# One averaging product per group norm, an earlier range count, and moved fill-in work in the last stretch of a four-layer kernel

## The chip, the cores and the metric

The kernel runs on one core of a Trainium2 chip. The time is the device time of one launch in microseconds (us); the figure compared is the median of several runs. Before the change it was 2970.94 us (three runs, 2970.92 to 2973.89). Names used below: PE is the matrix engine (TensorE), DVE the vector engine, ACT the scalar engine, POOL the GpSimd engine, SP the engine that issues most DMAs. A bank is one 128 x 512 float32 piece of PSUM, the accumulator memory that PE writes; there are eight.

## What is computed

Four images of 256 channels and 64 x 64 pixels go through four layers. Every layer adds f(group_norm(x)) to x, with groups of 8 channels. Cut to what matters:

```python
# layer 0: 3x3 convolution, group norm of 8 groups (32 channels each), relu, non-local attention, a second such norm
xs = relu(group_norm(conv3x3(xn) + smooth_b, gn1_w, gn1_b))
attn = softmax(theta(xs) @ phi(xs))            # 4096 x 4096 for each image
x = x + group_norm(conv1x1(attn @ g(xs), w_w) + w_b, gn2_w, gn2_b) * 0.1 + xs
# layer 1: rmsnorm, linear attention with 4 heads, rmsnorm
# layer 2: a small network makes a depthwise 3x3 kernel and a 1x1 kernel from the image itself
# layer 3: softmax over 4 experts mixes a 1x1 kernel
def _gn(v, G=32, eps=1e-5):                    # in front of every layer
    m = mean(group(v)); s = var(group(v))
    return (v - m) / sqrt(s + eps)
```

The softmax of layer 0 is taken without a running maximum. So the kernel counts on the way whether every sum and its reciprocal stayed in range, and a general version runs behind it if one did not.

## The kernel before

`conv_preact_fast` works on one image at a time, both halves of 128 channels (`NH = 2`) side by side on 128 partitions. While image b is in the attention of layer 0 (`attend`, L986), which keeps PE dense with products `pf` (L1013) and `py` (L1126, L1129), the other layers of image b-1 and the convolution of image b+1 are threaded into it step by step (`Chain`, L50, and the calls at L1989 to L1998). The program order on every engine is the order in which these Python generators emit: `tc.manual_schedule` (L1986) keeps it. Each engine runs its own list in order and waits on semaphores.

Two stretches have nothing beside them. The first image's convolution and norm (`convolve_first`, L863; `normed_relu`, L745) come before any attention. And the last image's layers 0 to 3 (`tail`, L1948, with `xs_in` and `diag` set, so that `alone` is true in the helpers) come after all of it. There the kernel fills PE's waits in two ways:

- **Held products.** The 16 pieces of image 2's layer 3 (`mixed`, L1927 to L1930) are not issued when they are ready but kept in a list, and `w.fill(n)` (L58) issues the next n: per piece four matrix passes of 512 columns (`ps_ex` L1907). `w.settle()` later issues their evictions on ACT, and these the stores on SP. All 16 have to be issued somewhere.
- **Dummies.** `warm(n)` (L350) issues 2n products of 128 x 128 of constants, four passes for each n, whose result nobody reads.

A group norm needs per-channel means and variances (`bn_stats` and `bn_aggr` on DVE, or sums that ACT and DVE accumulate on the way), then the average over the channels of a group. `group_finish` (L396) takes two products for that, one after the other: `pm` averages the means over the group (`avg32` or `avg8`, a block-diagonal matrix), DVE forms variance plus squared deviation from that mean, `pv` averages it, and POOL takes the power -0.5 (`rsqrt`, L230). Five such norms lie in the two lonely stretches: in `normed_relu` for image 0, and for the last image in `nonlocal_out` (L1152, whose statistics of the layer-0 sum are worked out from those of its parts: `wmv`, `res_mv`, `joint`), in `linear_attention` (L1261), in `generated` (L1521) and in `mixed` (L1840).

What surrounds them in the last image: `ended` (L1074) turns the last block of the attention (`ps_yt`, L1091), projects it (`ps_wy`, L1101) and takes its statistics (`wy_st`, L1030). At L2010 the loop over the rest of the attention's steps issues held products after the first of them. `linear_attention` runs eight blocks that transpose and project, forms the context (`ps_ctx`), turns it into one matrix `w2` by three small products (L1386 to L1402), and applies it in `outputs`, eight blocks, each adding into `big` with `bn_stats` beside it (`added`, L1439). `generated` plans its depthwise taps over four engines (`emit_by_start`, L1496). Its last sums are accumulated by `added` on DVE (L1769) and `square` on ACT (L1774). `mixed` then finds the mixing weights: norm, `ps_hid`, `ps_log`, softmax, `wm` on DVE, and the 16 final products with evictions on ACT and DVE and stores on SP.

At the very end, outside, `conv_preact_kernel` (L2518) compares the collected `guard` values (`fit`, `low`), counts over the partitions by a product (`count`, L2536), makes an integer (`good`), loads it into a register of each engine (L2538) and branches around the general version (L2539). The list order on DVE lets `fit` and `low` run early, but `count` stands behind the last final product.

Of the kernel before, what the change touches and what calls it, by code (L numbers as in the profile page):

```python
# [13 lines left out]
P = 128  # L14
# [89 lines left out]
def conv_preact_fast(ctx: ExitStack, tc: tile.TileContext, guard, x, wc, wtpg, ww, wqkv, wout, w1cat, wd2,  # L104
# [252 lines left out]
    def sums_tile():  # L357
        return sp.tile([P, 2, NH, N // 512], F32, name="sums", bufs=1)
# [21 lines left out]
    def accumulated(sums, pivot, parts=N // 512):  # L380

        both = sp.tile([P, 2, NH], F32, name="both_m", bufs=1)
        mv = sp.tile([P, NH, 2], F32, name="mv")
        if parts == N // 512:
            nc.vector.tensor_reduce(both, sums, AX.X, ALU.add)
        else:
            nc.vector.tensor_reduce(both[:, 0, :], sums[:, 0, :, 0:parts], AX.X, ALU.add)
            nc.vector.tensor_reduce(both[:, 1, :], sums[:, 1, :, :], AX.X, ALU.add)
        nc.vector.tensor_scalar(both, both, 1.0 / N, None, ALU.mult)
        tt(pivot, pivot, both[:, 0, :], ALU.add)  # L390
        tt(pivot, pivot, pivot, ALU.mult)
        tt(mv[:, :, 1], both[:, 1, :], pivot, ALU.subtract)
        nc.vector.tensor_copy(mv[:, :, 0], both[:, 0, :])
        return mv

    def group_finish(st, avg, eps, shift=None, between=(), idle=(0, 0)):  # L396
# [34 lines left out]
        return mv, gm, rstd  # L431

# [312 lines left out]
    def normed_relu(b, st, hops=0):  # L745
# [4 lines left out]
        _, gm, rstd = yield from group_finish(st, avg32, 1e-5, bias, (), (0, 0) if b else (7, 1))  # L750
        if b == 0:
            warm(5)
# [110 lines left out]
    def convolve_first(w):  # L863
# [59 lines left out]

        for oh in range(NH):
# [3 lines left out]
            nc.vector.tensor_scalar(minus[:, oh:oh + 1], pivot[:, oh, 0:1], -1.0, None, ALU.mult)  # L928
            for k in (1, 2):
                for i, f in enumerate((AF.Identity, AF.Square)):  # L930
                    nc.scalar.activation(k4("about").rearrange("p (y x) -> p y x", x=HW), image[:, oh, :, k, :], f,
                                         bias=minus[:, oh:oh + 1], accum_out=sums[:, i, oh, k - 1:k])
        for i, (y, ps) in enumerate(y3):
            tt(y, y, ps, ALU.add)
            if i == NH:
                half(0, 3)
        half(1, 3)

        yield from normed_relu(0, lambda: joined_moments(st, sums, minus))
# [32 lines left out]
    pivot_in = cp.tile([P, NH], F32, name="pivot_in")  # L972
    last_block, res_mv = [], []
# [4 lines left out]
    def residual_known():  # L978
# [5 lines left out]
        tt(res_shift, res_mv[0][:, :, 0], factors[:, 1, :], ALU.add)  # L984

    def attend(b):  # L986
# [8 lines left out]
        def with_residual(q, wt, xc):  # L995

            if q == 0:
# [3 lines left out]
                nc.vector.tensor_scalar(pivot_in, mv[:, :, 0], -1.0, None, ALU.mult)  # L1001
            if q < NQ - 1:
# [149 lines left out]
    def nonlocal_out(w, b, big, k4, xs_in):  # L1152
# [22 lines left out]
        wmv, gm, rstd = yield from group_finish(wy_stats[b], avg32, 1e-5, bias, between, (0, 0) if xs_in is None else (2, 1))  # L1175
# [6 lines left out]
        if xs_in is not None:  # L1182


            mean = sp.tile([P, NH, 1], F32, name="mean_in", bufs=1)
# [5 lines left out]
            rmv = res_mv[0]  # L1191
            tt(off, wmv[:, :, 0], pivot_in, ALU.add)
            tt(off, off, bias, ALU.subtract)
            nc.vector.tensor_reduce(cov, joint, AX.X, ALU.add)
            tt(off, off, rmv[:, :, 0], ALU.mult)
            stt(cov, cov, 1.0 / N, off, ALU.mult, ALU.subtract)
            tt(off, wmv[:, :, 0], gm, ALU.subtract)
            tt(sc, rstd, factors[:, 0, :], ALU.mult)
            tt(off, off, sc, ALU.mult)
            tt(mean[:, :, 0], off, res_shift, ALU.add)  # L1200
            w.fill(1)

            def variance():
                tt(var, wmv[:, :, 1], sc, ALU.mult)
                stt(var, cov, 2.0, var, ALU.mult, ALU.add)
                tt(var, var, sc, ALU.mult)
                tt(var, var, rmv[:, :, 1], ALU.add)
                return var
# [25 lines left out]
            return (lambda: (mean, variance)), (sh, shift), on_the_way()  # L1234
# [26 lines left out]
    def linear_attention(w, b, big, qT, k4, st, sh, sums):  # L1261

        alone = sums is not None
        if alone:
# [6 lines left out]
            _, gm, rstd = yield from group_finish(st, avg8, 1e-5, None, (lambda: next(sums), at_last), (0, 1))  # L1271
# [88 lines left out]
        for c in range(NC):  # L1360
            if c + 1 < NC:
                ahead = normed(c + 1)
            if alone:
                next(sums, None)
            elif b + 2 < B and c % 2 == 0:
                copy_x(b + 2, c // 2)
# [20 lines left out]
        for h in range(NH):  # L1387
            nc.tensor.transpose(pt[:, bass.ts(h, P)], cx[:, bass.ts(h, P)], ident)
        cxT = k2("cxT")[:, 0:NH * P]
# [3 lines left out]
        for h in range(NH):  # L1393
            nc.tensor.matmul(pe[:, 0:P], wqkv_s[:, h, 2 * HID:3 * HID], cxT[:, bass.ts(h, P)], start=(h == 0), stop=(h == NH - 1))
        cmT = k2("cmT")[:, 0:P]
# [4 lines left out]
        nc.tensor.matmul(pw[:, 0:NH * P], cmT, wout_s, start=True, stop=True)  # L1400
        w2 = k2("w2")[:, 0:NH * P]
# [46 lines left out]
        if alone:  # L1448

            this, last = outputs(0), None  # L1450
            root(this[0])
            for c in range(NC):
# [4 lines left out]
                if last is not None:  # L1457
                    added(c - 1, last)
                this, last = after, z
                w.settle()  # L1460
                if c in (2, 4):
# [5 lines left out]
            return st  # L1467
# [53 lines left out]
    def generated(w, b, big, k4, st, sh, diag):  # L1521
# [4 lines left out]
        mv, gm, rstd = yield from group_finish(st, avg8, 1e-5, sh, (), (0, 0) if diag is None else (0, 1))  # L1526
        if diag is not None:
            w.fill(1)

        pivot = sp.tile([P, NH], F32, name="pivot", bufs=1)  # L1530
        tt(pivot, sh, mv[:, :, 0], ALU.subtract)
# [66 lines left out]
        sums = sums_tile()  # L1598

        def st():  # L1600
            return accumulated(sums, pivot)
# [231 lines left out]
        else:  # L1833
            yield from halves_of_three()
        sh2 = sp.tile([P, NH], F32, name="sh2")
# [4 lines left out]
    def mixed(w, b, big, k4, st, sh, held):  # L1840
# [4 lines left out]
        alone = held is None and b == B - 1  # L1845
        if alone:
            w.fill(1)
        mv, gm, rstd = yield from group_finish(st, avg8, 1e-5, sh, (), (0, 1) if alone else (0, 0))
        if alone:
            warm(2)  # L1850
        off = sp.tile([P, NH], F32, name="off")
        tt(off, gm, sh, ALU.subtract)
        pool = sp.tile([P, NH], F32, name="rpool", bufs=1)
        tt(pool, mv[:, :, 0], gm, ALU.subtract)
        tt(pool, pool, rstd, ALU.mult)
# [20 lines left out]
        w.fill(3)  # L1876

        scales = sp.tile([P, NH, NE], F32, name="scales", bufs=1)
        for h in range(NH):
            nc.vector.tensor_scalar(scales[:, h, :], al, rstd[:, h:h + 1], None, ALU.mult)  # L1880
# [66 lines left out]

    def tail(b, big, qT, k4=k4, diag=None, xs_in=None, held=None):  # L1948
# [37 lines left out]
    with tc.manual_schedule(engines={E.PE, E.Activation, E.DVE, E.Pool, E.SP}):  # L1986
# [23 lines left out]
        for part, _ in enumerate(attention):  # L2010
            if part == 0:
                end.fill(2)
# [505 lines left out]
def conv_preact_kernel(ctx: ExitStack, tc: tile.TileContext, *args):  # L2518
# [4 lines left out]
    conv_preact_fast(tc, guard, *args)  # L2523


    fit = gp.tile([P, 2, B * NQ + 1], F32, name="fit")
    for side in range(2):
        nc.vector.tensor_scalar(fit[:, side, :], guard[:, side, :], GUARD_MAX[side], None, ALU.is_le)
    low = gp.tile([P, 1], F32, name="low")
    nc.vector.tensor_reduce(low, fit.rearrange("p s k -> p (s k)"), AX.X, ALU.min)  # L2530
    every = gp.tile([P, 32], F32, name="every")
    nc.gpsimd.memset(every, 1.0)
    good = gp.tile([32, 1], mybir.dt.int32, name="good")
    with tc.tile_pool(name="guard_ps", bufs=1, space=bass.MemoryType.PSUM) as gps:
        count = gps.tile([32, 1], F32, name="count")
        nc.tensor.matmul(count, every, low, start=True, stop=True)  # L2536
        nc.vector.tensor_scalar(good, count, P - 0.5, None, ALU.is_ge)
    in_range = nc.values_load(good[0:1, 0:1], min_val=0, max_val=1)  # L2538
    with tc.If(in_range < 1):  # L2539
# [59 lines left out]
```

## Time and profile before

| what | us |
|---|---|
| median of three runs | 2970.94 (2970.92 to 2973.89) |
| the profiled execution's own time | 2974.19 |
| its span, first to last instruction | 2972.4 |
| PE busy | 2918.3 (98%) |
| DVE, ACT, POOL busy | 1785.9, 1352.4, 187.1 |
| first image's last row product to first projection (`ps_tp`) | 130.4 to 140.2 |
| last image alone, from the turn of its last attention block to the last product | 2732.8 to 2964.3 |
| from the last product to the end of the span | 8.1 |

The profile is of one execution. Its span leaves out 1.8 us of its own time. Busy times of PE come from modelled ends of pipelined passes: in a dense stream a pass of 512 columns starts every 0.43 us, one of 128 columns every 0.11 us at full clock. The granted clock is a record of its own, in fractions of full speed. A group of instructions in the timeline is given by start, duration, engine, source line, operation, tiles written and read, and, where the engine stood idle before it, how long and what released it. Helpers such as `tt` (L137) and `stt` (L140) give all their instructions one line, so that a DVE operation is best followed by its tiles.

### The profile page before, as it was taken

The numbers are of one execution on the slowest core, as the hardware profiler recorded it, in microseconds if no ns is written. First come the engines' busy times: TensorE is split into PE (matmuls) and PEld (weight loads), VectorE is DVE, ScalarE is ACT, GpSimd is POOL, SyncE is SP. The second block draws the span as 40 slices with busy tenths as digits, with TensorE's granted clock in tenths as the row PEclk, the third lists the DMA queues.
The fourth block names the chain that finished last, engine by engine and source line by source line (L and its number), as shares of the span: only waits on it lengthen the run. The fifth ranks groups of instructions, "written<-read, shape, count | busy, mean of one in ns | idle before, by whom it ended". The sixth has DMA issues, their size and how long they took to land.

```text
span 2972.4 us, 31260 instructions
## 1 busy us (share of the span) xinstructions
PE 2918.3 (98%) x11604; PEld 1776.5 (60%) x11604; DVE 1785.9 (60%) x2793; ACT 1352.4 (45%) x2717; POOL 187.1 (6%) x225
## 2 busy tenths in 40 slices
PE   7999999999999999999999999999999999999998
PEld 3454555556566666777566666677646544446744
DVE  8737757751545853675355584567244558863584
ACT  2234333345656444225665544323656554433773
POOL 0000000001001000000011000000001100000152
PEclk9999999999999999999999999999999999999999
DMA  6245444324322012121630302211431233235121
GB/s 228 73 87 120 70 62 76 45 32 100 114 39 36 29 78 75 53 62 28 156 75 4 58 7 107 68 50 57 83 102 14 25 43 39 32 58 116 36 71 72
DMA packets 371296, 199.38 MB, mean 67 GB/s; under 512 B 305664, under 2 KB 315648, under 8 KB 367616
## 3 DMA queue, kind: packets, MB, share of 16 engines
q1 hardware_dynamic: 71328, 175.81, 17.6%
q10 hardware_dynamic: 295200, 4.72, 8.0%
q0 software_dynamic: 4608, 16.78, 3.8%
q8 instruction: 93, 1.52, 0.2%
q14 instruction: 67, 0.55, 0.1%
HBM read 131.18 MB, written 82.87 MB: 72 GB/s over the span
## 4 chain that ended last, share of the span: by engine, by line
PE 78%; issue 16%; DVE 3%; ACT 2%; DMA 1%; POOL 0%; SPq 0%; DVEq 0%; ACTq 0%; POOLq 0%
PE pf L1013 24%; PE py L1129 16%; PE py L1126 8%; PE ps_tp L951 4%; PE ps_qk L1316 3%; PE ps_ex L1907 3%; PE ps_pw L1620 3%; PE ps_conv L663 2%; PE ps_ctx L1343 2%; PE ps_o L1414 2%; PE ps_g L956 2%; PE ps_row L617 1%; PE ps_conv L578 1%; PE ps_wy L1066 1%; ACT big L760 1%
## 5 line engine op out<-in xcount | busy, mean ns | idle before, releaser
L1014 ACT ACTIVATE pr<-pf 128x512 f32<-128x512 f32 x1024 | 602.3, 596 | 911.7 <-PE pf L1013 888.9
L1013 PE MATMUL pf<-tpg 128*128 128x512 f32 x2048 | 966.4, 594 | 0.0
L1013 PEld LDWEIGHTS pf<-tpg 128*128 128x128 f32 x2048 | 374.1, 190 | 358.4 <-issue 336.4
L1129 PE MATMUL py<-pr,tpg 128*128 128x512 f32 x1152 | 541.6, 592 | 0.9 <-ACT pr L1014 0.9
L1126 PEld LDWEIGHTS py<-tpg,pr 128*128 128x128 f32 x3584 | 434.9, 192 | 108.0 <-issue 100.7
L1126 PE MATMUL py<-tpg,pr 128*128 128x129 f32 x3584 | 436.3, 275 | 2.3 <-ACT pr L1014 2.3
L1129 PEld LDWEIGHTS py<-pr,tpg 128*128 128x128 f32 x1152 | 218.6, 190 | 277.5 <-issue 268.3
L137 DVE TENSOR_TENSOR tot<-tot,pr 128x1024 f32<-128x1024 f32 x252 | 307.5, 1220 | 98.6 <-ACT pr L1014 98.1
L140 DVE SCALAR_TENSOR_TENSOR dw<-xp,dk,dw 128x1008 f32<-128x1008 f32 x192 | 242.9, 1270 | 7.6 <-ACT dw L1612 2.4
L663 PE MATMUL ps_conv<-v,u 128*128 128x256 f32 x864 | 195.6, 379 | 2.4 <-DVE v L137 2.4
L663 PEld LDWEIGHTS ps_conv<-v,u 128*128 128x128 f32 x864 | 161.5, 190 | 31.4 <-issue 8.4
L232 POOL TENSOR_TENSOR rstd<-rstd,half 128x2 f32<-128x2 f32 x24 | 17.5, 730 | 2093.8 <-DVE rstd L427 1983.4
L951 PE MATMUL ps_tp<-big,wtpg_s 128*128 128x512 f32 x256 | 116.7, 595 | 4.0 <-ACT big L760 4.0
L137 DVE TENSOR_TENSOR tpg<-ps_g,bg_s 128x512 f32<-128x512 f32 x32 | 22.1, 691 | 155.6 <-PE ps_g L956 155.6
L1316 PE MATMUL ps_qk<-wqkv_s,xg 128*128 128x256 f32 x496 | 113.6, 379 | 0.0
L140 DVE SCALAR_TENSOR_TENSOR sums<-ps_conv,sums 128x512 f32<-128x512 f32 x72 | 49.7, 691 | 104.0 <-PE ps_conv L663 97.6
L1316 PEld LDWEIGHTS ps_qk<-wqkv_s,xg 128*128 128x128 f32 x496 | 93.8, 190 | 20.3 <-issue 8.4
L1620 PE MATMUL ps_pw<-dw,pk 128*128 128x512 f32 x192 | 86.3, 592 | 0.0
L951 PEld LDWEIGHTS ps_tp<-big,wtpg_s 128*128 128x128 f32 x256 | 45.9, 190 | 53.4 <-issue 42.1
L952 ACT ACTIVATE tpg<-ps_tp,btp_s 128x512 f32<-128x512 f32 x64 | 44.0, 687 | 70.8 <-PE ps_tp L951 70.8
L1079 DVE COPY total<-py 128x2 f32<-128x2 f32 x28 | 4.5, 159 | 115.6 <-PE py L1126 115.6
L1915 ACT ACTIVATE res<-ps_ex,b 128x512 f32<-128x512 f32 x56 | 38.1, 686 | 75.3 <-PE ps_ex L1907 74.4
(412 smaller groups left out, 3351.6 us busy)
## 6 DMA issues: line engine op xcount, KB each, us to landing
u<-filters SPq DMA_DIRECT2D x72, 256.0 KB, 2.8
xp<-in_x_dram SPq DMA_DIRECT2D x16, 1024.0 KB, 8.3
xs_d<-big POOLq DMA_DIRECT2D x32, 512.0 KB, 6.3
wy_d<-wt SPq DMA_DIRECT2D x32, 512.0 KB, 2.8
wy<-wy_d SPq DMA_DIRECT2D x32, 512.0 KB, 4.9
out_dram<-res SPq DMA_DIRECT2D x64, 256.0 KB, 2.0
xs_d<-in_x_dram SPq DMA_DIRECT2D x24, 512.0 KB, 6.7
xs<-xs_d SPq DMA_DIRECT2D x24, 512.0 KB, 5.5
```

What stands on the lines that cost most here:

```text
L137: nc.vector.tensor_tensor(o, a, b, op)
L140: nc.vector.scalar_tensor_tensor(o, a, s, b, op0, op1)
L663: nc.tensor.matmul(ps[:, bass.ts(oh, IY * IX)], u[i][:, h, bass.ts(oh, P)], v[:, i, bass.ts(h, IY * IX)], start=(h == 0), stop=(h == NH - 1))
L951: nc.tensor.matmul(ps, wtpg_s[:, h, k, :], big[:, h, cols], start=(h == 0), stop=(h == NH - 1))
L956: nc.tensor.matmul(ps[:, j, :], big[:, h, bass.ts(4 * c + j, P)], wtpg_s[:, h, 2, :], start=(h == 0), stop=(h == NH - 1))
L1013: nc.tensor.matmul(pf, phi[:, bass.ts(2 * m + s, P)], theta[:, bass.ts(q, 512)], start=True, stop=True)
L1014: nc.scalar.activation(pr[:, bass.ts(s, 512)], pf, AF.Exp)
L1126: nc.tensor.matmul(py[t // 2][:, t % 2, :], probs[i][:, s * 512 + t * P:s * 512 + (t + 1) * P], g[:, 2 * m + s, :], start=(begin and t % 2 ...
L1129: nc.tensor.matmul(py, g[:, 2 * m + s, 0:P], probs[i][:, bass.ts(s, 512)], start=begin, stop=end)
L1316: nc.tensor.matmul(ps[:, 0:2 * HID], xg[:, h, bass.ts(j, P)], wqkv_s[:, h, 0:2 * HID], start=(h == 0), stop=(h == NH - 1))
L1620: nc.tensor.matmul(ps, pk[:, h * NH * P + oh * P:h * NH * P + (oh + 1) * P], dw[h][:, bass.ts(s, 512)], start=(h == 0), stop=(h == NH - 1))
L1907: nc.tensor.matmul(ps, wm[h][:, bass.ts(oh, P)], big[:, h, bass.ts(c, 512)], start=(h == 0), stop=(h == NH - 1))
```

## The change

Five norms get one averaging product in place of two. `group_once` and `group_known` put mean and variance-plus-square into one tile, both taken about a value that all channels of a group have in common (`centre`), and average the two in one product. Group variance is then the averaged square minus the square of the averaged mean. The common value is averaged earlier by a small product of its own: from the first quarter of the image in `convolve_first`, from the first block in `attend` and in the outputs of layer 1, and from the residual's mean in `residual_centred`.

```diff
+    def group_known(both, centre, avg, eps, between=(), idle=0):
+        yield None
+        warm(idle)
+        pm = bank("pm")
+        nc.tensor.matmul(pm[:, 0:2 * NH], avg, both.rearrange("p k h -> p (k h)"), start=True, stop=True)
+        for f in between[0:1]:
+            f()
+        sq = sp.tile([P, NH], F32, name="sq_g", bufs=1)
+        nc.vector.tensor_copy(sq, pm[:, 0:NH])
+        tt(sq, sq, sq, ALU.mult)
+        rstd = sp.tile([P, NH], F32, name="rstd")
+        stt(rstd, pm[:, NH:2 * NH], eps, sq, ALU.add, ALU.subtract)
+        rsqrt(rstd, rstd)
+        gm = sp.tile([P, NH], F32, name="gm")
+        tt(gm, pm[:, 0:NH], centre, ALU.add)
...
     def normed_relu(b, st, hops=0):
-        _, gm, rstd = yield from group_finish(st, avg32, 1e-5, bias, (), (0, 0) if b else (7, 1))
         if b == 0:
-            warm(5)
+            gm, rstd = yield from group_known(*st(), avg32, 1e-5, (), 7)
+            warm(6)
+        else:
+            _, gm, rstd = yield from group_finish(st, avg32, 1e-5, bias)
...
# convolve_first, between the sums that ACT accumulates for the second half of the channels
+                    if oh == 1 and k == 1 and i == 1:
+                        centre = centre_of(shifted, avg32, nc.scalar.copy)
+                        nc.gpsimd.tensor_tensor(off, bias, centre, ALU.subtract)
...
```

In `convolve_first` a new function `moments` (ten steps on DVE behind the two `bn_aggr`, the reduction of ACT's sums first) takes the place of `joined_moments`. In `nonlocal_out` the residual's variance is worked out ahead of the product instead of beside it. In `mixed` the sums are averaged as they are, unscaled, and `rstd` is kept in another unit that `scales` takes back:

```diff
 # nonlocal_out
-        wmv, gm, rstd = yield from group_finish(wy_stats[b], avg32, 1e-5, bias, between, (0, 0) if xs_in is None else (2, 1))
+            wmv = aggregated(wy_stats[b])
+            gm, rstd = yield from group_once(wmv, wy_minus, wy_centre, avg32, 1e-5, between, 3)
+            w.fill(2)
...
-            w.fill(1)
...
 # linear_attention
-            _, gm, rstd = yield from group_finish(st, avg8, 1e-5, None, (lambda: next(sums), at_last), (0, 1))
+            gm, rstd = yield from group_known(st, res_centre, avg8, 1e-5, (lambda: next(sums), at_last))
...
+                if c == 2:
+                    checks.append(counted())
+                if c in (2, 4, 5):
+                    next(checks[0])
...
# after the products ps_cx, ps_cm and ps_w2, if alone: warm(1), warm(1), warm(2)
...
-                if c in (2, 4):
+                if c in (2, 4, 6):
                     w.fill(1)
...
 # generated
-        mv, gm, rstd = yield from group_finish(st, avg8, 1e-5, sh, (), (0, 0) if diag is None else (0, 1))
-        if diag is not None:
+            gm, rstd = yield from group_once(mv, minus, centre, avg8, 1e-5, (), 0)
             w.fill(1)
...
+        if diag is not None:
+            nc.gpsimd.tensor_scalar(sums[:, 0, :, N // 512], pivot, float(N), None, ALU.mult)
+            nc.gpsimd.memset(sums[:, 1, :, N // 512:N // 512 + 1], N * 1e-5)
...
 # mixed
         if alone:
             w.fill(1)
-        mv, gm, rstd = yield from group_finish(st, avg8, 1e-5, sh, (), (0, 1) if alone else (0, 0))
-        if alone:
-            warm(2)
+            warm(3)
+            st, pivot = st
+            both = sp.tile([P, 2, NH], F32, name="both_c", bufs=1)
+            loaded()
+            nc.vector.tensor_reduce(both, st, AX.X, ALU.add)
+            pm = bank("pm")
+            nc.tensor.matmul(pm[:, 0:2 * NH], avg8, both.rearrange("p k h -> p (k h)"), start=True, stop=True)
+            warm(5)
...
-        w.fill(3)
+        w.fill(2 if alone else 3)
...
 # the calls at the end
             if part == 0:
-                end.fill(2)
+                residual_centred()
+                warm(2)
+            else:
+                end.fill(1)
```

The range check moves inside. `counted` does the comparisons at block 2 of layer 1's loop, the counting product at block 4 and the integer at block 5; `loaded` loads the register in `mixed`. The branch stays where it was:

```diff
+    def counted():
+        fit = k2("fit")[:, 0:2 * (B * NQ + 1)].rearrange("p (s k) -> p s k", s=2)
+        for side in range(2):
+            nc.vector.tensor_scalar(fit[:, side, :], guard[:, side, :], GUARD_MAX[side], None, ALU.is_le)
+        low = sp.tile([P, 1], F32, name="low", bufs=1)
+        nc.vector.tensor_reduce(low, fit.rearrange("p s k -> p (s k)"), AX.X, ALU.min)
+        yield
+        count = bank("count")
+        nc.tensor.matmul(count[0:32, 0:1], ones[:, 0:32], low, start=True, stop=True)
+        yield
+        nc.vector.tensor_scalar(good, count[0:32, 0:1], P - 0.5, None, ALU.is_ge)
+        yield
+    def loaded():
+        in_range.append(nc.values_load(good[0:1, 0:1], min_val=0, max_val=1))
...
-    in_range = nc.values_load(good[0:1, 0:1], min_val=0, max_val=1)
-    with tc.If(in_range < 1):
+    with tc.If(in_range[0] < 1):
         conv_preact_general(tc, *args)
```

The held products after the change: 1 at the calls, 2 in `nonlocal_out`, 1 before and 1 after layer 1's loop, 3 in the outputs and 3 behind them, 2 in `generated`, 1 and 2 in `mixed`: 16 again.

## Prediction

> **What bounds the kernel now.** I read the totals first, then the chain of waits, then windows and the timeline of the last 240 us. TensorE (PE) is busy 98% of the span: until image 3's attention ends (2732 us) it has no gap to fill, so what the change does to shared code there is worth little. The time is in stretches where PE waits for a chain of tiny operations. Windows 2720 to 2964.3 hold 244.3 us with PE busy for 228.4: 15.9 us of gaps at most, plus 8.1 us after the last product, plus what a halved clock costs. The clock is seen only in windows laid on its changes (from:to, length, busy us and count per engine, granted clock):
>
> ```profile
> core 0: us, PE busy (x) PEld busy (x) DVE busy (x) ACT busy (x) POOL busy (x), PEclk, DMA share, GB/s
> 132.80:136.21 3.41, 1.76 (x15) 1.44 (x13) 2.21 (x17) 0.00 (x0) 0.00 (x0) 1.00 0.01 2
> 136.21:139.62 3.41, 3.41 (x17) 3.41 (x17) 0.71 (x5) 1.40 (x2) 0.70 (x1) 0.50 0.02 5
> 2743.99:2747.41 3.42, 2.47 (x12) 1.60 (x12) 3.11 (x17) 0.69 (x1) 0.57 (x1) 1.00 0.20 77
> 2921.49:2924.90 3.41, 1.85 (x9) 0.84 (x7) 1.72 (x11) 0.76 (x2) 0.00 (x0) 1.00 0.00 0
> 2924.90:2931.73 6.83, 6.83 (x23) 5.15 (x24) 2.58 (x14) 0.93 (x3) 0.71 (x1) 0.50 0.05 17
> ```
>
> Two windows with PE busy 1.76 and 1.85 us of 3.41 were followed by half clock; one with 2.47 was not. The second halving is dear. The timeline there (start, us, engine, line, operation, idle before):
>
> ```profile
> 2922.28 0.18 DVE L385 TENSOR_REDUCE both_m<-sums 128x4 f32<-128x32 f32 x1 [0.87 <-ACT junk L1775]
> ...
> 2923.58 0.38 PE L409 MATMUL pm<-mv,avg 128*128 128x2 f32 x2 [1.27 <-DVE mv L137]
> 2923.83 0.69 PE L355 MATMUL ps_warm<-ident,ones 128*128 128x128 f32 x4
> ...
> 2924.81 0.53 PE L425 MATMUL pv<-ev,avg 128*128 128x2 f32 x2 [0.29 <-DVE ev L137]
> 2925.20 2.05 PE L355 MATMUL ps_warm<-ident,ones 128*128 128x128 f32 x8
> ...
> 2927.18 0.59 PE L1859 MATMUL ps_hid<-rpool,rw_s 128*64 128x1 f32 x4
> ...
> 2929.36 6.57 PE L1907 MATMUL ps_ex<-big,wmh 128*128 128x512 f32 x12
> ```
>
> Eight dummies take 2.05 us here and 1.06 us at 2838.55; `rpool` is ready at 2926.51 and waits for them until 2927.18. The end, by the load's and the If's lines:
>
> ```profile
> L2538 DVEq TENSOR_LOAD <-good x1: 819/819/819, 2965.7 to 2965.7; - x1
> L2538 PEldq TENSOR_LOAD <-good x1: 796/796/796, 2965.7 to 2965.7; - x1
> ...
> L2539 PEldq COMPARE_BRANCH  x1: 4672/4672/4672, 2966.6 to 2966.6; - x1
> ...
> L2539 DVEq EVENT_SEMAPHORE  x1: 21/21/21, 2970.3 to 2970.3; - x1
> ```
>
> The last product is done at 2964.30 and the last result at 2965.14, but every engine loads the verdict before it branches, and PE is back from its branch only at 2971.3.
>
> **The change, part by part** (times in us of the profiled run; minus is a gain).
>
> A, first image's norm. The old DVE chain from the last squares (small steps start 0.195 apart when dependent, 0.08 when not) runs 132.64 to 134.62; the new `moments` has nine dependent links after its first reduce, 2.1, and starts later: `centre`'s copy sits on ACT between the squares, must wait for PE's row products (end 130.4) and its own product (0.35), so ACT's last two squares slip 0.5. Then one PE turn (0.55) is gone. Relu starts near 137.97 instead of 138.22: -0.25 on ACT, up to -0.7 on PE, whose first tpg product is held till 140.21 by slow dummies. The 2.3 us gap before `pm` makes half clock likely again, and six dummies more would then end at 140.3, as now. Bounds -0.7 to +0.5, taken -0.3, nearest to the halved row.
>
> Attention of image 3: one tiny product among dense ones, three small DVE steps under ACT/PE cover: +0.2 (0 to 0.3, by the 0.17 to 0.37 of `pm` rows).
>
> B, image 3's second norm and the next one. Now the chain is PE:
>
> ```profile
> 2732.81 0.64 PE ps_yt L1091 x4
> 2733.45 3.44 PE ps_ex L1907 x8
> 2736.88 1.73 PE ps_wy L1101 x4
> ```
>
> `yt` is ready at 2734.31, yet `ps_wy` starts at 2736.72, behind two held products. With a small product and `warm(2)` (8 x 0.11) there instead, `ps_wy` starts near 2734.4, 2.3 earlier. `wy_st` and `mv` follow at unchanged distance (2738.1); three DVE steps instead of one put `pm` at 2738.85, but fill(1) and `warm(3)` (12 x 0.11) hold it to 2739.2. Squared mean, variance and power end near 2741.4; the residual's small steps, now with variance ahead of the product, let the second `pm` go at 2743.4 (was 2744.80), its power ends at 2745.8 (was 2747.91), and DVE normalises at 2746.4 (was 2748.31). ACT normalises at 2746.4 instead of 2748.97, because the last held eviction (2748.39) is earlier too. PE's transposes: 2747.25 against 2749.83, with four held products done in both. -2.5; if DVE's `multiply` and the POOL power (1.04 here, 0.71 alone) collide worse, -1.5; best -2.8.
>
> Attention loop of layer 1: the count's two compares and a reduce (0.27 + 0.22, rows of 2732.8) on DVE, a 32-column product, one compare. DVE idles 1.1 to 1.4 in most blocks: 0 to +0.6, taken +0.3. A PSUM bank is out for one block.
>
> Around `w2`: dummies of 0.44, 0.44, 0.88 in PE gaps of 0.46, 0.38 and 0.52. Only the last outgrows its gap: +0.2 (0 to 0.4).
>
> C, outputs and layer 2's norm. A held product at c = 6 falls into idle of 1.14 and 0.26 before and in `ps_zt`; the DVE chain that ends the stage waits for `rt` (2837.88) anyway: 0 (to +0.3). ACT's and POOL's small `early`/`centre` steps: +0.2. The norm: old one + PE + four + PE + one DVE steps, new three + PE + three, so one PE turn goes: power at 2848.7, not 2849.20. The held product starts after the first `pm`, so PE is free for `ps_b` at 2849.85, not 2850.67: -0.8. Together -0.6. POOL's two new steps on `sums` run long before its taps (idle 10.66 before 2860.60).
>
> D, layer 3's norm. Seven DVE steps before `pm` become one (data at 2922.46), but PE has the held product to 2922.15 and `warm(3)` to 2923.5: `pm` hardly moves. Then three DVE steps (0.6), power (0.8), `rpool` (0.2): 2925.5; `warm(5)` at full clock ends 2926.0. `ps_hid` 2926.0 (was 2927.18), 0.59, DVE 0.5, `ps_log` ends 2927.65 (was 2929.43). From there DVE needs 3.59 to the first mixed half (2933.02 - 2929.43), so 2931.25; two held products end at 2931.1. First final product 2931.3 against 2935.77: -4.4. Of this 1.7 is the product moved to C's cover. The new register load stands on all five queues: on DVE in the 0.87 idle before the reduce, on PE behind `warm(3)` with `pm` behind it; if PE's queue does not read ahead, +0.8. ACT's next is the Exp at 2929.67, SP's a store at 2930.63.
>
> Here the skill argues against the dummies. The page "TensorE: Matmul & The Clock Gate", "What's actually happening", has the clock halve only after a whole idle window of about 3.4 us. No gap here reaches 1.3, so by that rule the dummies buy nothing. Working the old chain at full clock (`ps_hid` 2926.45, `ps_log` to 2928.1, three held products 5.16 to 2933.3), D would gain 2.0. The rows show halving at 52% and 54% busy, so for the profiled run I take 4.4.
>
> E, the end. The load (0.8, and 0.55 of `count` and `good`) leaves the end; the branch stays. "Runtime: NRT & Kernel Launch", "Instruction fetch mechanics", says a taken branch out of the instruction window must fetch its target, so the stall itself remains; the trace agrees: ACT is away 3.0, DVE 3.7, PE 4.67, all at once. What moves is its start: PE 2964.35 or sooner, DVE 2964.4 to 2965.2. If each keeps its stall PE is back at 2969.0, -2.3; if apart each takes ACT's 3.0, DVE is back at 2968.2 or less, -3.1; the last store lands at 2967.17 and bounds it at -3.9. Taken -3.0.
>
> Sum: -0.3 +0.2 -2.5 +0.3 +0.2 -0.6 -4.4 -3.0 = -10.1; 2974.19 - 10.1 = 2964.1. The profiled run is 3.25 over the median, and the other runs are 2970.92 to 2973.89. I read half clock in D (2.4) as most of this. Against the median the sum is -7.7: 2963.2. I say 2963.6.
>
> **Rivals.** (1) The load is not read ahead, the exit keeps PE's full stall and B's DVE steps collide: 2963.6 + 0.8 + 0.7 + 1.0 = 2966.1. For it: DVE is nearly without gaps in B; against: the sequencers issue ahead elsewhere. (2) The stalls at the end overlap with the last store wholly, and A stays at full clock: 2963.6 - 0.9 - 0.4 - 0.5 (B best) = 2961.8. (3) The count holds a bank in layer 1's loop and PE loses half a block of 6.5: 2966.9; against: its next user comes a block later. (4) Slower: the clock halves at `pm` in D and stays so into the final products, 1.7 lost per 3.41 us. It decides beyond 4.3 windows (7.3 / 1.7); six give 2973.8. For it: one halving there lasted two windows; against: dense products ended it, and the new order leaves PE about 60% busy.
>
> **How the numbers follow.** Forecast 0.5 (2961.5 to 2965.5), rivals 0.2, 0.2, 0.05, 0.05. The range, 2960.0 to 2968.0, takes in the bounds up to rival 3. 0.2% is 5.9 us, the least this measurement tells from none: faster means under 2965.0, which is most of the forecast, all of rival 2 and little of rival 1: 0.70; slower 0.04.
>
> **What would show it.** Right: no half clock after 2900; `ps_wy` straight behind dummies; first `ps_ex` on `wm` 8 us earlier; no load after the last result, and under 6 us from last product to end. Wrong: `pm` in D waiting on the load, half clock in a window of the tail, or a branch stall grown past 4.7.

## The result, and the profile after

| | before | after | |
|---|---|---|---|
| median of 14 runs each | 2973.85 us (2970.92 to 2974.68) | 2965.20 us (2964.60 to 2965.66) | ratio 0.9973, 95% interval 0.9966 to 0.9981 |
| the profiled execution, own time | 2974.19 us | 2965.21 us | -8.98 |
| its span | 2972.4 us | 2963.3 us | -9.1 |

The kernel is 0.27% faster. The prediction was 2963.6 us with a range of 2960.0 to 2968.0: the side and the range held, the time was 1.6 us too low. The runs of before lie in two groups, here four at 2970.92 to 2971.05 and ten at 2973.03 to 2974.68; the median of three runs that the prediction started from, 2970.94, was of the lower group, the profiled run of the upper one. Against the lower group the gain is 5.8 us. Where each step landed is read from the start of the same instruction in both traces (the last column is by how much the distance to the step ahead of it changed):

| step, and the mark at its end | before | after | predicted | measured |
|---|---|---|---|---|
| A, third `ps_tp` | 141.07 | 140.71 | -0.3 | -0.36 |
| image 3's attention, first `ps_yt` of the last stage | 2732.79 | 2732.66 | +0.2 | +0.23 |
| B, first `ps_xt` | 2749.83 | 2746.91 | -2.5 | -2.79 |
| loop of layer 1, `ps_cx` | 2806.52 | 2803.96 | +0.3 | +0.36 |
| around `w2`, first `ps_o` | 2809.67 | 2807.32 | +0.2 | +0.21 |
| C, `ps_b` of layer 2 | 2850.67 | 2848.70 | -0.6 | **+0.38** |
| D, first final product | 2935.77 | 2929.15 | -4.4 | -4.65 |
| E, end of the last product to the end | 8.11 | 5.59 | -3.0 | **-2.52** |

All but C and E agree within 0.3 us. First the windows of the changed kernel, laid on the changes of the clock (from:to, length; busy us and count of PE, of its weight loads PEld, of DVE, ACT and POOL; granted clock, DMA share, GB/s):

```profile
132.73:136.14 3.41, 1.73 (x16) 1.57 (x15) 2.34 (x18) 0.07 (x1) 0.00 (x0) 1.00 0.01 2
136.14:139.55 3.41, 3.41 (x19) 3.41 (x18) 0.67 (x6) 1.81 (x2) 0.95 (x2) 0.50 0.03 7
2918.01:2921.42 3.41, 3.41 (x18) 2.19 (x17) 0.89 (x3) 1.36 (x4) 0.00 (x0) 1.00 0.01 5
2921.42:2924.83 3.41, 3.41 (x33) 3.27 (x31) 1.29 (x9) 0.00 (x0) 0.73 (x1) 1.00 0.01 2
```

The halving in A is still there, behind a window with 1.73 us of PE. In D both windows are full and the clock stays at 1.00. The next fence is the timeline of B (start, us, engine, line, operation, idle before it):

```profile
2732.66 0.66 PE L1179 MATMUL ps_yt<-ident,yn 128*128 128x128 f32 x4 [0.93 <-DVE yn L137]
2733.16 0.28 PE L1064 MATMUL pm_c<-res_shift,avg 128*128 128x2 f32 x2
2733.30 1.14 PE L355 MATMUL ps_warm<-ident,ones 128*128 128x128 f32 x8
...
2734.27 1.95 PE L1189 MATMUL ps_wy<-yt,ww_s 128*128 128x512 f32 x4
```

`ps_wy` stands straight behind the dummies, at 2734.27 where the sum had 2734.4. The timeline of D in the changed kernel:

```profile
2920.37 0.19 DVE L1977 TENSOR_REDUCE both_c<-sums 128x4 f32<-128x36 f32 x1 [1.01 <-ACT junk L1895]
...
2921.52 0.28 PE L1979 MATMUL pm<-both_c,avg 128*128 128x4 f32 x2
...
2921.66 2.48 PE L355 MATMUL ps_warm<-ident,ones 128*128 128x128 f32 x20
...
2924.07 0.39 PE L2001 MATMUL ps_hid<-rpool,rw_s 128*64 128x1 f32 x4
...
2925.34 3.70 PE L2052 MATMUL ps_ex<-big,wmh 128*128 128x512 f32 x8
...
2929.15 2.38 PE L2052 MATMUL ps_ex<-tpg,wm 128*128 128x512 f32 x5
```

One `pm` instead of two turns, `both_c` ready at 2920.56 but `pm` held by `warm(3)` until 2921.52, and then two held products instead of three. Last, the instructions of the load (L2113), and of the If (L2697) and what lies behind it (L2753); the times are duration min/median/max in ns and first and last start in us:

```profile
L2113 PEldq TENSOR_LOAD <-good x1: 487/487/487, 2917.6 to 2917.6; - x1
L2113 DVEq TENSOR_LOAD <-good x1: 535/535/535, 2918.7 to 2918.7; - x1
```

```profile
L2697 SPq EVENT_SEMAPHORE  x8: 17/17/17, 2961.1 to 2961.6; - x8
...
L2697 PEldq COMPARE_BRANCH  x1: 3424/3424/3424, 2949.9 to 2949.9; - x1
...
L2697 DVEq COMPARE_BRANCH  x1: 76/76/76, 2957.9 to 2957.9; - x1
...
L2697 DVEq EVENT_SEMAPHORE  x1: 21/21/21, 2960.7 to 2960.7; - x1
```

```profile
L2753 SPq EVENT_SEMAPHORE  x14: 17/28/28, 2961.7 to 2963.3; - x14
```

PE and DVE read the register while PE was still on the products ahead of `pm` (2921.52): the load is off the path. PE's sequencer took its branch at 2949.9, 7.8 us before its last product was done (2957.75), so its stall is gone from the end. DVE branches at 2957.9 and is back at 2960.7. But SP, which waits for the stores one semaphore after another, only begins at 2961.1, when the last one has landed, and is through at 2963.3: it now ends the kernel. Before, the same row held waits of up to 1.55 us for the engines that were still in their branches:

```profile
L2595 SPq EVENT_SEMAPHORE  x14: 17/28/1549, 2968.2 to 2972.3; - x14
```

C's loss is all at one place, block 4 of the outputs loop. Just ahead of it PE stands 2.44 us earlier than before, behind it 1.22:

```profile
2824.47 1.08 PE L1545 MATMUL ps_zt<-ident,z 128*128 128x128 f32 x8
...
2825.39 0.28 PE L467 MATMUL pm_c<-early,avg 128*128 128x2 f32 x2
...
2825.71 0.73 DVE L140 SCALAR_TENSOR_TENSOR tpg<-ps_zt,gains,tpg 128x512 f32<-128x512 f32 x1
...
2826.49 1.98 PE L2052 MATMUL ps_ex<-big,wmh 128*128 128x512 f32 x4 [0.82 <-DVE tpg L140]
...
2828.32 1.89 PE L1515 MATMUL ps_o<-w,tpg 128*128 128x256 f32 x8
```

The held product waits 0.82 us for DVE to finish reading a `ps_zt` (2825.71 + 0.73 = 2826.44), though it has nothing to do with that data. Both tiles come from the eight PSUM banks that `bank` hands out in turn. Before, the held product followed `ps_zt` without a wait:

```profile
2826.91 1.08 PE L1444 MATMUL ps_zt<-ident,z 128*128 128x128 f32 x8
2827.82 1.88 PE L1907 MATMUL ps_ex<-big,wmh 128*128 128x512 f32 x4
```

### The profile page after: what moved, and what is told of

Same layout as the page of the kernel before. It is cut to its first block, busy times and chain, and to the rows that moved or that the text cites. A ratio compares the mean times of both kernels' runs of the same rounds, so it can differ in the third digit from the quotient of the medians.

```text
span 2963.3 us, 31330 instructions
## 1 busy us (share of the span) xinstructions
PE 2917.0 (98%) x11638; PEld 1777.7 (60%) x11638; DVE 1786.2 (60%) x2792; ACT 1353.8 (46%) x2720; POOL 189.4 (6%) x235
## 5 line engine op out<-in xcount | busy, mean ns | idle before, releaser
L1417 ACT ACTIVATE qk<-ps_qk,rinv 128x256 f32<-128x256 f32 x100 | 46.6, 474 | 56.1 <-PE ps_qk L1407 51.9
```

The source lines that it names most:

```text
L1417: nc.scalar.activation(qk[:, j, :], ps[:, 0:2 * HID], AF.Exp, scale=rinv[:, j:j + 1])
```

## The experiments

Three questions: is C's loss the bank, or the small steps; what do the held products, their order, the check and the dummies of the other steps weigh each; and does the clock go by the share of a window or by whole idle windows.

**e1, the bank.** `pm_c` goes behind the held product:

```diff
-                if c == 4:
-                    centre = centre_of(early, avg8, lambda o, i: nc.scalar.mul(o, i, 0.5))
-                    nc.gpsimd.tensor_tensor(early, sh, centre, ALU.subtract)
                 this, last = after, z
                 w.settle()
                 if c in (2, 4, 6):
                     w.fill(1)
+                if c == 4:
+                    centre = centre_of(early, avg8, lambda o, i: nc.scalar.mul(o, i, 0.5))
+                    nc.gpsimd.tensor_tensor(early, sh, centre, ALU.subtract)
```

> The product for `centre` and the held product of block 4 in the outputs loop change places: the held product goes first, `pm_c` behind it. Nothing else. Theory (banks): in the changed kernel `pm_c` takes the PSUM bank that was the next to come free, and the held product gets the following one, which DVE reads until 2826.44; so PE stands 0.82 us and the held product starts 1.2 late. With the order turned the held product follows the transposes directly, `pm_c` finds its bank free behind it, and everything after moves 1.2 us earlier: 2964.0 instead of 2965.2, with the held product of block 4 starting within 0.1 us of the end of `ps_zt`. Rival (steps): the 1.2 us are the time of the small steps themselves, ACT's copy of 0.19, POOL's 0.20 and PE's 0.28, which are still there: no change, 2965.2 within 0.3.

Measured: 2963.72 us (2963.53 to 2964.16, 8 runs), where the changed kernel has 2965.20 in the result above and 2964.95 (2964.73 to 2965.71, 10 runs) when it ran once more with e4, e6 and e7 on another chip (label c_after). From the timeline of e1:

```profile
2824.44 1.08 PE L1545 MATMUL ps_zt<-ident,z 128*128 128x128 f32 x8
2825.36 1.88 PE L2052 MATMUL ps_ex<-big,wmh 128*128 128x512 f32 x4
2827.08 0.28 PE L467 MATMUL pm_c<-early,avg 128*128 128x2 f32 x2
2827.22 1.97 PE L1515 MATMUL ps_o<-w,tpg 128*128 128x256 f32 x8
```

The same instructions, the held product without a wait, `ps_o` at 2827.22 instead of 2828.32, and the end of the stage 1.02 earlier. All small steps are still there, so the rival is out: the price was the bank. What is left of the 1.22 us is the small product's own place on PE.

**e2, the moved product.** The held product of block 6 goes back to `mixed`:

```diff
-                if c in (2, 4, 6):
+                if c in (2, 4):
...
-        w.fill(2 if alone else 3)
+        w.fill(3)
```

> The held product of block 6 in the outputs loop goes back to `mixed` (three there again instead of two). Theory: in the outputs loop it stands in idle time and costs nothing, and in `mixed` the third product (1.72 us) keeps PE beyond the time when `wm` is ready (2929.0): the final products start 2925.3 + 5.4 = 2930.7 instead of 2929.15, and the whole is +1.5, 2966.7; the marks at the end of the outputs loop stay within 0.2. Rival: the product in the loop costs as much as in `mixed`, so the loop gets shorter by what `mixed` gets longer: 2965.2 within 0.3.

Measured: 2966.15 us (2965.89 to 2966.78, 14 runs). The last `bn_stats` of the outputs loop keeps its distance to all marks ahead of it (-0.17 on each), so the product costs the loop nothing. In `mixed`:

```profile
2925.18 5.42 PE L2052 MATMUL ps_ex<-big,wmh 128*128 128x512 f32 x12
...
2930.43 1.88 PE L2052 MATMUL ps_ex<-tpg,wm 128*128 128x512 f32 x4
```

The first final product comes 1.45 us later against the mark ahead. The move is worth 1.45 of D's 4.65, where the sum had 1.7, and the rival (a product that costs the same in both places) is out.

**e3, the check at the end.** The count leaves the loop of layer 1 and runs with its load behind the last eviction:

```diff
-                if c == 2:
-                    checks.append(counted())
-                if c in (2, 4, 5):
-                    next(checks[0])
...
-            loaded()
...
         assert not held and not end.unsettled
+        for _ in counted():
+            pass
+        loaded()
```

> The range check runs at the end again, behind the last eviction, all of it, with its load; the loop of layer 1 is without it. The scratch tile of the comparisons is another one. Theory: the end grows by the load and by the branches that all come at once, 2.5 us as the two traces differ, and the loop of layer 1 gives back 0.36: +2.1, 2967.3. In the loop the mark `ps_cx` comes 0.3 to 0.4 earlier. Rival: the small loss in the loop is not the count's but the rotated banks' or chance, so `ps_cx` does not move and the whole is +2.5, 2967.7. Second rival: what the end gained came from the order of the queue, not from the load; then it is +0.5 or less.

Measured: 2966.76 us (2966.31 to 2967.38, 20 runs). In the trace the loop of layer 1 is 0.36 us shorter and the end 2.49 longer: +2.13, as the theory had it. The medians differ by less, 1.6 and 1.8 (from the two medians of the changed kernel). The If's lines of e3:

```profile
L2695 PEldq COMPARE_BRANCH  x1: 4392/4392/4392, 2959.2 to 2959.2; - x1
...
L2695 PEldq EVENT_SEMAPHORE  x1: 51/51/51, 2963.7 to 2963.7; - x1
```

PE's branch, 4.39 us and now behind the load, ends the kernel again. Laid ahead, it costs nothing at the end.

**e4, no dummies in `mixed`.** `warm(3)`, `warm(5)` and `warm(1)` are left out.

> The changed kernel without the dummy products in `mixed` (3 + 5 + 1, 36 small products, 4.2 us of PE). Theory (clock by share): from 2920.2 to the held products PE then has only 1.05 us of work in some 4 us, less than the share at which the clock was halved before; half clock comes in every run, the two held products take up to 6.9 us instead of 3.4, and what the earlier `pm` and `ps_hid` gain (1.5) is more than lost: 2965.7 to 2968.5, with a half-clock stretch after 2920. Rival (the page's rule): no gap is a whole window, the clock stays, and `pm`, `ps_hid` and the first final product come 0.9 to 1.5 earlier: 2963.7.

Measured: 2965.05 us (2964.04 to 2966.07, 10 runs), the same as with them. The windows of e4 on its clock changes, and a line of its timeline:

```profile
2920.25:2923.66 3.41, 1.22 (x9) 1.02 (x10) 1.49 (x10) 0.00 (x0) 0.73 (x1) 1.00 0.02 5
2923.66:2927.07 3.41, 3.41 (x5) 1.33 (x6) 2.77 (x11) 0.93 (x3) 0.00 (x0) 0.50 0.19 77
2927.07:2930.48 3.41, 3.41 (x10) 1.50 (x9) 2.08 (x6) 1.37 (x2) 0.00 (x0) 1.00 0.20 79
```

```profile
2923.49 5.40 PE L2048 MATMUL ps_ex<-big,wmh 128*128 128x512 f32 x8
```

Both theories missed the time, and each was half right. The clock does halve, behind a window with 1.22 us of PE, and with no gap over 1.64 us: by the rule that the prediction weighed (the Trainium skill, "TensorE: Matmul & The Clock Gate", "What's actually happening") it would not, at 2963.7. But the halving lasted one window, not two: the held products took 5.40 instead of 3.70 us, and that gave back the 1.38 us by which `ps_log` had come earlier than in c_after. The first final product stands at +0.04 against c_after.

**e5, dummies in the kernel before.** One number in the kernel before:

```diff
-        mv, gm, rstd = yield from group_finish(st, avg8, 1e-5, sh, (), (0, 1) if alone else (0, 0))
+        mv, gm, rstd = yield from group_finish(st, avg8, 1e-5, sh, (), (2, 1) if alone else (0, 0))
```

> The kernel before with one edit: eight dummy products (idle 2 instead of 0) ahead of `pm` in `mixed`, in a gap of 1.27 us where PE has nothing. It adds 0.88 us of work to the window 2921.49 to 2924.90, which was 1.85 busy, and none to the path. Theory (clock by share of busy time): 2.73 of 3.41 is more than the 2.47 that kept the clock, so half clock does not come, and all runs are where the kernel before has its fastest: 2971.0, none at 2973 to 2974.7. Rival (the page's rule, a whole idle window): the dummies do nothing, and the runs are spread over 2971 to 2974.7 as before, or up to 0.2 later. Second rival: the spread of 3 us comes from another place; then the half clock near 2924.9 is gone and the runs at 2973 to 2974.7 stay.

Measured: 2970.89 us (2970.34 to 2972.55, 13 runs, twelve of them up to 2971.54); the kernel before in 46 runs of that chip has 21 from 2970.08 to 2971.20, one at 2971.86, and 24 from 2972.82 to 2975.23. The upper group is gone; one run, 2972.55, lies between the groups. (As a ratio to the kernel before: 0.9996, 95% interval 0.9988 to 1.0004, so a gain over all runs is not shown; the change is in how they spread.) The windows of e5:

```profile
2921.70:2925.11 3.41, 2.75 (x19) 2.13 (x18) 1.72 (x11) 0.48 (x2) 0.00 (x0) 1.00 0.02 5
2925.11:2928.52 3.41, 3.17 (x21) 2.43 (x21) 1.20 (x8) 0.54 (x3) 0.71 (x1) 1.00 0.00 0
```

With 2.75 us of PE in the window the clock stays, and against the profiled run of before the first final product comes 2.8 us earlier. So work that computes nothing took the slower group from the kernel before, and the rule of a whole idle window doesn't hold here: without the dummies the longest gap there was 1.27 us.

**e6, the order in B.** The held products stand where they were, the new norm stays:

```diff
                 residual_centred()
-                warm(2)
-            else:
-                end.fill(1)
+                end.fill(2)
...
-            w.fill(2)
+            w.fill(1)
```

> The changed kernel with the held products of stage B where they were: two ahead of `ps_wy` in place of the dummies, one behind the attention, one (not two) in `nonlocal_out`; the one-turn norm stays. Theory: the order on PE is nearly all of B's gain. `ps_wy` starts at 2737 instead of 2734.4 and all behind it is 2.3 to 2.6 later: 2967.6. Rival: the gain is the norm's (one PE turn and one power less on the path), and the products only change places: 2965.2 to 2965.8.

Measured: 2968.07 us (2967.09 to 2969.02, 20 runs). The timeline of e6:

```profile
2733.09 3.68 PE L2052 MATMUL ps_ex<-big,wmh 128*128 128x512 f32 x8
...
2736.61 1.88 PE L1189 MATMUL ps_wy<-yt,ww_s 128*128 128x512 f32 x4
```

`ps_wy` waits behind the products again, and from `ps_yt` to `ps_xt` e6 takes 2.28 us longer than c_after (2.55 against 0.27 later); all marks behind keep that. With the new norm in place the order is thus worth 2.3 of B's 2.79, and 0.5 is left for the norm.

**e7 and c_after, a version from the findings, and the changed kernel beside it.** The core of the edit, on top of that of e1:

```diff
# around w2
         if alone:
-            warm(1)
+            next(checks[0])
         cmT = k2("cmT")[:, 0:P]
...
-            warm(2)
+            warm(1)
...
+        if alone:
+            next(checks[0])
# mixed
-            warm(5)
+            warm(3)
+            nc.vector.tensor_scalar(rstd, rstd, rstd_unit, None, ALU.mult)
-                nc.vector.tensor_scalar(scales[:, h, :], al, rstd[:, h:h + 1], rstd_unit, ALU.mult, ALU.mult)
+                nc.vector.tensor_scalar(scales[:, h, :], al, rstd[:, h:h + 1], asum, ALU.mult, ALU.mult)
+                if j == 0 and h == 1 and alone:
+                    nc.scalar.activation(wm[h], e, AF.Copy, scale=scales[:, h, 0:1])
# the last block: two products of 256 columns
+        nc.scalar.activation(res[:, 0:256], halves[0][:, 0:256], AF.Identity, bias=b3[:, oh:oh + 1])
+        nc.vector.tensor_scalar(res[:, 256:512], halves[1][:, 0:256], b3[:, oh:oh + 1], None, ALU.add)
```

> A version from the findings: `pm_c` behind the held product (-1.0); the counting product and its compare moved out of the busy loop to the place of a dummy around `w2` (-0.3), the last dummies there 1 instead of 2 (-0.2); in `mixed` 3 instead of 5 ahead of `ps_hid` (-0.5 on PE's path), the division by the sum of exponentials folded into the scales (-0.2), the first term of the second mixed matrix on ACT (-0.3 at most); the last block's product in two column halves, evicted by ACT and DVE and stored apart (-0.3). Sum -2.5: 2962.7. Rival for the end: the last store and SP's row of waits set the end, so the halves gain only what the last eviction gains, 0.3, or lose if two stores land later than one. Rival for `mixed`: with fewer dummies the clock is halved there and the version is at 2965 or more in some runs.

> The changed kernel as it is, beside the others on their chip: 2964.6 to 2965.7.

Measured: e7 2962.46 us (2962.30 to 2963.34, 6 runs), c_after 2964.95 (2964.73 to 2965.71, 10 runs): -2.5, as summed. By the marks against c_after, the loop of layer 1 gains 0.36 (its whole loss, so it was the counting product on a full PE and the one compare behind it), `w2` and C 1.12, D 0.78, the end 0.47. The profiled run of e7 starts its last stage 0.7 later than that of c_after, 0.47 of it by half clock in A: c_after has none. The windows of c_after in A, laid in steps of 3.413 us from its first full speed:

```profile
131.47:134.88 3.41, 2.07 (x19) 1.88 (x17) 2.80 (x15) 1.30 (x4) 0.00 (x0) 1.00 0.00 0
134.88:138.29 3.41, 3.07 (x26) 2.98 (x26) 1.27 (x9) 0.58 (x1) 0.70 (x1) 1.00 0.03 7
```

**e8 and e7 again, the row of waits.** On e7, four earlier stores are cut in halves, and 1 instead of 3 times four dummies stand ahead of `pm`:

```diff
-            warm(3)
+            warm(1)
             st, pivot = st
...
+                if b == B - 1 and 4 <= c < 6:
+                    def halves():
+                        for s in range(2):
+                            nc.sync.dma_start(out=out[b, bass.ts(oh, P), c * 512 + s * 256:c * 512 + s * 256 + 256],
+                                              in_=res[:, s * 256:s * 256 + 256])
+                    return halves
```

> Two edits on the version of e7. First, four earlier stores of the last image are cut in two halves each, so that the last store signals the eighth of the eight semaphores that SP waits for in a row, not the fourth. Theory (SP's row): what follows the last landing is SP's waits one after another, 0.065 to 0.07 us each, so with four waits fewer behind the landing the time from landing to the end is 0.25 to 0.3 shorter than in e7 (1.95 there, 2.22 in the changed kernel with the first semaphore): 1.65 to 1.7. Rival (fixed): the time from landing to the end does not depend on which semaphore it is, 1.95. Second, dummies of 1 instead of 3 ahead of `pm` in `mixed`: PE sets the first final product there, so it comes 0.85 earlier (0.4 if the mixed matrix is late) with the clock at full; rival: half clock comes back. Sum against e7: -1.1, 2961.4.

> The version of e7 again, beside e8 on the same chip: 2962.3 to 2963.3.

Measured: e8 2961.35 us (2960.60 to 2961.72, 5 runs), e7 again 2962.43 (2962.09 to 2962.94, 6 runs). From the last landing to the end of the span: 2.27 us in the changed kernel (2961.07 to 2963.34), 2.00 in e7 again (2958.36 to 2960.36), 1.72 in e8 (2958.21 to 2959.93), steps of 0.27 and 0.28, as foretold. SP's waits of e8:

```profile
L2720 SPq EVENT_SEMAPHORE  x8: 17/17/17, 2956.8 to 2958.2; - x8
```

Seven of the eight were through before the last landing at 2958.21. But cutting the stores made SP's last issue later, and the last store lands 3.70 us behind the start of the last product instead of 3.47, so the end as a whole gains only 0.05. Of the 1.08 us between the medians the marks of the two profiled runs show 0.81, and 0.79 of that is D's; the rest stays open. `pm` starts at 2919.32 there, 0.06 behind its data (2919.26), and the clock stays:

```profile
2919.32 0.38 PE L1980 MATMUL pm<-both_c,avg 128*128 128x4 f32 x2
...
2926.28 3.67 PE L2057 MATMUL ps_ex<-tpg,wm 128*128 128x512 f32 x8
```

e8 is the best of all: 3.6 us under the changed kernel.

## Why the prediction was right, and where it was wrong

**A** (-0.3, measured -0.36) was right, for an execution with half clock in both, and that part was luck: the gap ahead of `pm` that was to bring the half clock is 1.68 us, not 2.3, and in c_after the clock stays. Rival 2's other case is real too: the same kernel was profiled with and without half clock there, after and c_after, e7 and e7 again, and `ps_yt` comes 0.47 us earlier without (2732.66 and 2732.19, 2732.89 and 2732.43).

**B** (-2.5, measured -2.79) was right in mechanism and size; e6 gives 2.3 of it to the order, as the step said of `ps_wy`.

**The loop of layer 1 and `w2`** (+0.5, measured +0.57) were right in size. The loop's loss is neither DVE's compares at block 2 nor a lost half block (rival 3). All of it appears at block 4, where the counting product stands, and the blocks behind it, while its bank is out, lose nothing more; e7 moves the product into a gap and gets all of it back.

**C failed**, in the sentence "ACT's and POOL's small `early`/`centre` steps: +0.2". The norm itself did what the sum said (from the end of the loop to `ps_b`, -0.76 for -0.8), and the held product at block 6 cost nothing (e2). What the step put at nothing is the bank that `centre_of` takes. The next tile then gets the following one, and the held product waits for a reader of other data: +1.2 at one spot, 1.02 of it back by turning two instructions round (e1). The prediction weighed a bank in the loop of layer 1, where it cost nothing, and not here.

**D** (-4.4, measured -4.65) was right step by step: `ps_hid` at 2926.04 (2926.0 foretold) when the shift of the marks ahead of D, 1.97, is taken off, the first final product at 2931.12 (2931.3). The sign "first `ps_ex` on `wm` 8 us earlier" was not met, with 6.6; the prediction's own sum up to there is 7.1. The moved product is 1.45 of D (e2); the register load was read ahead (rival 1 is out). Rival 4, a halving that stays, is out: even without dummies one window was all (e4).

The half clock in D ("2.4") measured 2.8 (e5), and it is a chance, not a cost that every run bears: by their times 24 of 46 runs of before bear it, though only one such run was profiled. It goes with the spread of 3 us in before, which is 1 us after. For the lower group, without it, the prediction summed -7.7 and the gain is 5.8.

Of the two rules weighed, the whole idle window is out: halving came after windows of 3.41 us with PE busy for 1.22, 1.73, 1.76 and 1.85 us. Above them the clock stayed at 2.07, 2.47 and 2.75, as a rule by busy share would have it, but that rule is not the whole either. In layer 2 of the changed kernel, and at the end of e2 and of e1, windows with 1.88, 1.46 and 1.60 us kept the clock:

```profile
2853.15:2856.57 3.42, 1.88 (x10) 0.76 (x7) 1.23 (x5) 2.55 (x5) 0.00 (x0) 1.00 0.00 0
2856.57:2859.98 3.41, 2.41 (x7) 0.87 (x6) 3.23 (x7) 2.76 (x7) 1.26 (x1) 1.00 0.02 5
```

```profile
2957.49:2960.90 3.41, 1.46 (x4) 0.38 (x2) 0.75 (x1) 0.47 (x1) 0.00 (x0) 1.00 0.42 161
2960.90:2964.31 3.41, 0.00 (x0) 0.00 (x0) 0.00 (x0) 0.00 (x0) 0.00 (x0) 1.00 0.15 58
```

These windows hold mostly passes of 512 columns; in the four that halved, a good part of the busy time belongs to products of a few columns. An estimate from the same traces: count every pass by what it takes in a dense stream, 0.43 us for 512 columns and 0.11 for 128. Then every full-speed window of the twelve traces that was followed by half clock has at most 1.23 us, and every one that was not has at least 1.29. A few records can be missing from a trace, and no run varied this alone, so the edge is not exact and the rule not shown; it is the one that no trace here contradicts.

**E failed in size** (-3.0, measured -2.52). The branch stalls came apart as said, and PE's vanished from the end altogether, so that what ends the kernel is the term that was only a bound, "the last store lands at 2967.17 and bounds it at -3.9". It was mis-sized twice. It leaves 1.34 us from landing to end (the landing 2.87 behind the last product, 8.11 - 3.9 = 4.21); SP's row took 2.27, and 1.72 to 2.00 with the last store's semaphore later in the row (e8, e7 again). And the store took 2.45 us instead of 2.00. Why is not shown by a run of its own. In the trace of the changed kernel three packets of an instruction queue lie beside those of the store, between 2958.85 and 2960.55; in before and in e3, where the branches come later and the store took 2.00, there is none beside it.

C missed by 0.98 and E by 0.48; the other steps, with +0.07 for the final products, gave 0.4 back, and the profiled run is 1.1 above the sum (2965.2 for 2964.1). The forecast lay another 0.5 lower, as a middle between that sum and the one for the lower group. So errors of both signs are in the number, and the median stayed 0.2 above the 2965.0 under which the prediction put 0.70.

## What to carry to other kernels

A tiny product set into a full loop can cost, beside its 0.3 us, the buffer that it takes: count the rotation, and put it behind the big product whose bank it would take. Dummies pay only until a window of the clock holds enough work, here by the estimate 1.2 to 1.3 us of dense passes in 3.41; beyond that each delays the chain it guards. The busy time of tiny products is no measure of that. When the load of a verdict is moved far ahead of the end, look for what ends next: the last store, and the engine that waits for all stores one by one.

## What the hardware showed that was not expected

- The clock changes on a grid of 3.413 us (the length of the shortest halvings) that does not start with the kernel: from its first full speed to the halving in A it is 112.64 us, 33 steps, in every run that halves (23.50 to 136.14 in the changed kernel), while the start lies between 21.9 and 24.0 us of the span. The seven profiled executions with it at 23.1 or later halved in A, the five at 22.3 or earlier did not. So one and the same kernel has different times without any change in its work.
- PE's branch can be taken while PE still has 7.8 us of products ahead (2949.9, stall 3.42), and then adds nothing at the end; behind the products it cost 4.39 (e3) and 4.67 (before).
- SP's waits at the end cost 0.06 to 0.10 us each although all are met; which semaphore the last store has is worth up to 0.55 us.
